# Scans with a gate: moving VectorE's half gate by one product, and loading the gate's z chunks earlier into a ring of six

## The chip, the cores and the metric

The kernel runs on one core of one Trainium2 chip, in one launch. The metric is the device time of that launch in microseconds (us), taken as the median of several runs. The kernel of before takes 9846.35 us (three runs, 9833.42 to 9846.51). The profiled run that all lines below come from took 9824.87 us, with a span of 9823.0 us from the first to the last instruction.

## The reference, cut to what matters

Layer 0 is an attention block on an image batch of 8 x 128 x 128 x 128; its output feeds layer 1. Layer 1 is a two-dimensional selective scan. Its last part is what the change touches:

```python
delta = softplus(dt_weight[k] @ dt + dbias)          # per direction k of four
dA    = exp(delta * A)
xc    = dA * xc + (delta * u) * B                    # the scan, step by step over L = 16384
y     = xc * C
y     = y0 + y1 + y2 + y3                            # four directions, plus u * D
yz    = y * silu(z)                                  # the gate
yn    = gamma * (yz - mean) / sqrt(var + 1e-5) + beta
out   = yn @ Wout
```

There are 8 images, 256 inner channels (two halves of 128 partitions), and four scan directions for each image. silu(z) was computed in layer 0 and lies in HBM as `zs`.

## The kernel before

The program has three stages, one after the other: layer 0, the front of layer 1, and the scans (`layer1_scan`). The change is in the scans alone, which begin at about 5000 us and run to the end.

One *step* handles one chunk of 1024 positions of one direction of one image, both channel halves. 16 chunks make a direction (`NCH`), four directions make an image, 8 images follow each other: 512 steps, numbered n. The four directions of an image add into one tile `y` that stays in SBUF. The first direction of an image (place 0) writes `y`, so while it runs, the finished `y` of the image before must leave, chunk by chunk, just ahead of the writes. These 16 steps of each image are called *leaving steps* here; `leaving[n]` names the chunk that leaves in step n. Of the other places, two write `y` in turned order (the turned steps).

Nothing is left to a scheduler: `in_order` ties each engine's instructions to the order in which `step(n)` writes them. The order of one leaving step of before is:

- VectorE: `emit(n-1, 0)` and `emit(n-1, 1)` (the two products state x C of the step before, L917), `scan(n, 0)` (L889/L891), eight instructions of `store` for the chunk that left in the step before (L1019), `scan(n, 1)`, `state` (L899), `variance` (L1001), then its half of the gate for the next chunk (`gate(*soon, 1, nc.vector)`, L968).
- GpSimd (POOL): `weigh(n, 0)` (delta x u, L882), `deviation` (L1005, L1006), `weigh(n, 1)`, its own half of the gate for the next chunk (L968), and in some steps the issue of a DMA that adds the D term into `y` (`add_d`, L844).
- ScalarE (ACT): two `decay` (exponentials, L879), two squares of gated values (L971), a copy, two `soften` (softplus, L875), with a table load ahead of each kind.
- TensorE (PE): `moments` (L981), `delta` for step n+1 (L871), `to_tokens`, `spread` (L905), and `project` (32 matrix products, L1013), which reads both halves of z and writes into the PSUM tile that `scan(n, 1)` has finished with.
- The sync engine's queue (SP), which issues nearly all DMAs, in order, each after the semaphores that it waits for: `load_rows(n+2)` (L853, L854), `load(n+3)` (L860), the two `store` DMAs out<-r (L1023), and last the two `fetch` DMAs z<-zs (L964).

The buffers that matter: `z` is a ring of five tiles, and a chunk takes two, from `fetch` until `project` has read them. `r`, the output tile of `store`, is a ring of two, and both are used in every leaving step, so the store of a step needs the out DMAs of the step before to have landed. `sp` (the softplus result) is a ring of three. `px` in PSUM is a ring of three.

The schedule of the fetches before is written as

```python
fetched[n + j - 2 if j > 1 else n + j - 4] = e
```

where n is the image's first leaving step and j the number of the chunk: chunks 0 and 1 are fetched four and three steps ahead of the first leaving step, the others at the end of the step two ahead of their own.

Of the kernel before, what the change touches and what calls it, by code (L numbers as in the profile page):

```python
# [8 lines left out]
F32 = mybir.dt.float32  # L9
# [7 lines left out]
P = 128  # L17
# [4 lines left out]
NC2 = 2  # L22
R = 8
K = 4
GW = 4
GN = GW * H
# [3 lines left out]
CH = 1024  # L30
CW = CH // H
NCH = L // CH
# [7 lines left out]
def split3(nc, parts, x):  # L40

    for j in range(3):
        nc.vector.tensor_copy(parts[j], x)
        if j < 2:
            nc.vector.tensor_tensor(x, x, parts[j], ALU.subtract)
# [642 lines left out]
def layer1_scan(ctx: ExitStack, tc, ubs, xps, zs, gs, dtw, dtb, a_log, gamma, beta, w_out, out):  # L688
# [15 lines left out]
    nc = tc.nc  # L704
    const = ctx.enter_context(tc.tile_pool(name="l2c", bufs=1))
    big = ctx.enter_context(tc.tile_pool(name="l2b", bufs=1))
    wp = ctx.enter_context(tc.tile_pool(name="l2w", bufs=3))
# [14 lines left out]
    D2 = 2 * P  # L722
    wparts = dram.tile([3, R, K, D2], BF16, name="wparts")
    bparts = dram.tile([3, K, D2], BF16, name="bparts")
    for dst, src, rows in ((wparts, dtw.rearrange("k r d -> r k d"), R), (bparts, dtb.rearrange("o (k d) -> o k d", d=D2), 1)):
        x = wp.tile([rows, K, D2], F32, name="w32", tag="sp", bufs=3)
        nc.sync.dma_start(x, src)
        q = wp.tile([rows, 3, K, D2], BF16, name="w16", tag="ub", bufs=4)
        split3(nc, [q[:, j] for j in range(3)], x)
        for j in range(3):  # L730
            if rows == 1:
                nc.sync.dma_start(dst[j : j + 1], q[:, j])
            else:
                nc.sync.dma_start(dst[j], q[:, j])
# [8 lines left out]
    for i in range(3):  # L743
        t = const.tile([P, CH], BF16, name=f"rows{i}")
# [3 lines left out]
    for i in range(2):  # L748
        t = const.tile([P, D2], BF16, name=f"dtw{i}")
# [23 lines left out]
            nc.vector.memset(sel[at : at + 1, hf, j : j + 1], 1.0)  # L773
    pb = pe.tile([P, P], F32, name="pbw", tag="pt")
    for c in range(NC2):
        bt = wp.tile([P, P], F32, name="bt", tag="z", bufs=5)
        nc.vector.tensor_copy(bt, gb[:, 1, c : c + 1].to_broadcast([P, P]))
        nc.tensor.matmul(pb, bt, wg[:, c, :], start=(c == 0), stop=(c == NC2 - 1))
    bw = const.tile([P, P], F32, name="bw")
# [59 lines left out]
    ubt, sp, da, st = {}, {}, {}, {}  # L839
# [6 lines left out]
    def load_rows(n):  # L846
        sl, i = units[n]
        m = sl.at(i)
        rw = rws[n % 3]
        md = NCH - 1 - m if sl.dt_turned_back else m  # L850
        src = xps[sl.dt_image, sl.dt_order].rearrange("j r l -> (j r) l")
        for j in range(3):
            nc.sync.dma_start(rw[3 * NR * j : 3 * NR * j + 3 * NR, :], src[:, md * CH : md * CH + CH])  # L853
        nc.sync.dma_start(rw[96:99, :], xps[sl.b, sl.order, :, R + 1, m * CH : m * CH + CH])  # L854

    def load(n):
        sl, i = units[n]
        m = sl.at(i)
        ubt[n] = wp.tile([P, NC2, CH], F32, name="ubt", tag="ub", bufs=4)
        nc.sync.dma_start(ubt[n], ubs[sl.b, sl.order].rearrange("c p l -> p c l")[:, :, m * CH : m * CH + CH])  # L860
# [10 lines left out]
            nc.tensor.matmul(p[:, hf * 512 : hf * 512 + 512], sl.dw[:, c * P : c * P + P], src, start=True, stop=True)  # L871

    def soften(n, c):
        sp[n, c] = t = wp.tile([P, CH], F32, name="sp", tag="sp", bufs=3)
        nc.scalar.activation(t, da[n, c], AF.Softplus)  # L875

    def decay(n, c):
        sl, i = units[n]
        nc.scalar.activation(da[n, c], sp[n, c], AF.Exp, scale=sa[:, sl.s, c : c + 1])  # L879

    def weigh(n, c):
        nc.gpsimd.tensor_tensor(ubt[n][:, c, :], ubt[n][:, c, :], sp.pop((n, c)), ALU.mult)  # L882
# [24 lines left out]
    def emit(n, hf):  # L907

        sl, i = units[n]
        h = ubt[n][:, :, hf * 512 : hf * 512 + 512]
        c = cps.pop((n, hf)).to_broadcast([P, NC2, GN])
        if sl.place == 0:
            v = sl.y_at(i, hf)
            split = "p c (a b) -> p c a b"
            nc.vector.tensor_tensor(v, h.rearrange(split, b=H), c.rearrange(split, b=H), ALU.mult)  # L917
            if hf == 1:
                ubt.pop(n)
            return  # L920
        if hf == 1:
            nc.vector.tensor_tensor(h, h, c, ALU.mult)  # L922
            return
        p = da.pop((n, 1))
        if sl.y_turned:
            ts[n] = p.rearrange("p (c b a) -> p c b a", c=NC2, a=GW)
            t = p.rearrange("p (c b a) -> p c a b", c=NC2, a=GW)
            split = "p c (a b) -> p c a b"
            nc.vector.tensor_tensor(t, h.rearrange(split, b=H), c.rearrange(split, b=H), ALU.mult)  # L929
        else:  # L930
            t = p.rearrange("p (c q) -> p c q", c=NC2)
            ts[n] = t.rearrange("p c (a b) -> p c a b", b=H)
            nc.vector.tensor_tensor(t, h, c, ALU.mult)  # L933

    def gather(n):

        sl, i = units[n]
        v = sl.y_at(i, 0)
        if sl.y_turned:
            v = v.rearrange("p c a b -> p c b a")  # L940
        nc.vector.tensor_tensor(v, v, ts.pop(n), ALU.add)  # L941
# [9 lines left out]
    zt, rst, pts, mv = {}, {}, {}, {}  # L951

    def piece(m, hf):
        return y[:, :, (2 * m + hf) * GN : (2 * m + hf + 1) * GN]

    def mirrored(o, m, hf):
        p = 2 * m + hf
        return 2 * NCH - 1 - p if o % 2 == 1 else p

    def fetch(o, m):  # L960
        for hf in range(2):
            zt[m, hf] = z = wp.tile([P, NC2, GN], F32, name="z", bufs=5)
            p = mirrored(o, m, hf)
            nc.sync.dma_start(z, zs[o].rearrange("c p l -> p c l")[:, :, p * GN : p * GN + GN])  # L964

    def gate(o, m, hf, eng):
        z, ym = zt[m, hf], piece(m, hf)
        eng.tensor_tensor(z, ym[:, :, ::-1] if o % 2 == 1 else ym, z, ALU.mult)  # L968

    def square(m, hf):  # L970
        nc.scalar.activation(piece(m, hf), zt[m, hf], AF.Square)  # L971
# [31 lines left out]
    def deviation(m):  # L1003
        rstd = rst[m]
        nc.gpsimd.tensor_scalar(rstd, rstd, 0.0, EPS1, ALU.max, ALU.add)  # L1005
        nc.gpsimd.tensor_tensor(rstd, rstd, half, ALU.pow)  # L1006
# [20 lines left out]
    leaving, summed, fetched = {}, {}, {}  # L1027
    for o in range(B):
        n = (o + 1) * K * NCH
        for j in range(NCH):  # L1030
            e = o, NCH - 1 - j if o % 2 == 1 else j
            leaving[n + j] = e
            fetched[n + j - 2 if j > 1 else n + j - 4] = e
            summed[n - NCH + 3 + (3 * j + 1) // 2] = e
    N = len(units)

    def step(n):
        live = 0 <= n < N
        then = n + 1 < N
        before = 1 <= n <= N  # L1040
        now, last, soon = (leaving.get(n + i) for i in (0, -1, 1))
        first = before and units[n - 1][0].place == 0
        if before:
            emit(n - 1, 0)
            if not first:
                gather(n - 1)
            emit(n - 1, 1)
        if n + 2 < N:
            load_rows(n + 2)
        if first and n + 3 < N:  # L1050
            load(n + 3)
        if live:
            for c in range(NC2):
                decay(n, c)
            weigh(n, 0)
        if last:
            deviation(last[1])
        if live:
            weigh(n, 1)
        if now:  # L1060
            for hf in range(2):
                square(now[1], hf)
            moments(now[1])
        if live:
            scan(n, 0)
            da.pop((n, 0))
        if last:
            for hf in range(2):
                store(*last, hf)
        if then:  # L1070
            for c in range(NC2):
                delta(n + 1, c)
        if now:
            keep(now[1])
        if then:
            for c in range(NC2):
                soften(n + 1, c)
        if now:
            to_tokens(now[1])
            square_mean(now[1])  # L1080
        if live:
            scan(n, 1)
            state(n)
        if now:
            variance(now[1])
        if live:
            spread(n, 0, "pc")
            spread(n, 1, "pt")
        if soon:
            gate(*soon, 0, nc.gpsimd)  # L1090
            gate(*soon, 1, nc.vector)
        if now:
            p = da.pop((n, 1)) if live else px.tile([P, CH], F32, name="px")
            for hf in range(2):
                project(now[1], hf, p[:, hf * 512 : hf * 512 + 512])
        elif live and units[n][0].place == 0:
            da.pop((n, 1))
        if before and not first:
            add(n - 1)
        if n + 3 < N and not first:  # L1100
            load(n + 3)
        if live and units[n][1] == 1 and n - 1 + NCH < N:
            units[n - 1 + NCH][0].weights()
        if n in summed:
            add_d(*summed[n])
        if n in fetched:
            fetch(*fetched[n])

    with in_order(tc):
        units[0][0].weights()  # L1110
# [74 lines left out]
```

## Time and profile before

| what | value |
|---|---|
| median of 3 runs | 9846.35 us |
| VectorE busy, whole span | 8276.1 us (84%) |
| GpSimd busy | 7184.2 us (73%) |
| ScalarE busy | 7129.7 us (73%) |
| TensorE busy | 6386.5 us (65%) |
| DMA moved | 1851.21 MB, 188 GB/s over the span |
| VectorE's half gate (L968) | 128 instructions, mean 2233 ns |
| GpSimd's half gate (L968) | 128 instructions, mean 2380 ns |

Busy shares over the whole span mix three stages. What a change in the scans is worth is read from the windows of the scans, and there from the leaving steps apart from the turned ones. In a timeline line the columns are start, duration, engine, line, operation, output<-inputs, shape and count; in brackets stands how long the engine was idle before it, and what ended that.

### The profile page before, as it was taken

What the parts mean: (1) busy time and instruction counts of PE and PEld (TensorE: products, weight loads), DVE (VectorE), ACT (ScalarE), POOL (GpSimd) and SP (SyncE); (2) the same over time, 40 slices, a digit from 0 to 9 for tenths busy, and PEclk for the clock granted to TensorE, in tenths of its full rate; (3) what the DMA queues carried; (4) which work ended last, traced back from release to release, by engine and by line L of the source; (5) the groups of instructions that cost most, each with busy time, mean ns of one, the idle gap of its engine ahead of it and who ended that gap; (6) DMA issues with size and microseconds to landing.
All of it is one profiled execution on the core that took longest, in us unless ns stands there. A gap on an engine that the chain in (4) does not pass through costs nothing. (4 is left out here: it accounts for less than half of the span.)

```text
span 9823.0 us, 89967 instructions
## 1 busy us (share of the span) xinstructions
PE 6386.5 (65%) x24352; PEld 3135.3 (32%) x24352; DVE 8276.1 (84%) x8676; ACT 7129.7 (73%) x8226; POOL 7184.2 (73%) x4352
## 2 busy tenths in 40 slices
PE   8999999988787678667823544636345363553636
PEld 5555555553232223222300311404123040220403
DVE  6557775566898889888979999999999999999996
ACT  5556565556887788777778788887877878787784
POOL 3444554455484578667759899898998989889897
PEclk9999999999898889888955765757557585665857
DMA  2332233323666678877664957759587684866858
GB/s 91 129 131 97 86 118 131 129 101 132 219 221 214 219 265 228 243 248 263 232 197 152 253 177 202 234 164 263 154 223 207 176 257 152 246 185 191 239 153 215
DMA packets 1034807, 1851.21 MB, mean 188 GB/s; under 512 B 274852, under 2 KB 500772, under 8 KB 1026112
## 3 DMA queue, kind: packets, MB, share of 16 engines
q1 hardware_dynamic: 999488, 1711.23, 53.4%
q0 software_dynamic: 34816, 134.23, 7.1%
q8 instruction: 199, 3.26, 0.1%
q14 instruction: 304, 2.49, 0.1%
HBM read 1153.03 MB, written 692.12 MB: 188 GB/s over the span
## 5 line engine op out<-in xcount | busy, mean ns | idle before, releaser
L882 POOL TENSOR_TENSOR ubt<-ubt,sp 128x1024 f32<-128x1024 f32 x1024 | 2451.4, 2441 | 186.3 <-ACT sp L875 159.5
L871 PE MATMUL px<-rows,dtw 128*128 128x512 bf16 x2048 | 948.3, 564 | 2251.9 <-DVE y L941 1011.9
L504 POOL TENSOR_TENSOR tap<-tap 128x1024 f32<-128x1024 f32 x512 | 1206.2, 2366 | 720.7 <-ACT tap L502 614.7
L512 DVE SCALAR_TENSOR_TENSOR acc<-xb,cw,acc 128x1024 f32<-128x1024 f32 x1024 | 1320.7, 1290 | 51.1
L494 PE MATMUL acc<-xi,wt 128*128 128x512 f32 x2048 | 984.3, 625 | 570.8 <-ACT ures L519 570.5
L875 ACT ACTIVATE sp<-px 128x1024 f32<-128x1024 f32 x1024 | 1035.0, 1023 | 405.8 <-PE px L871 263.8
L948 POOL TENSOR_TENSOR y<-y,ubt 128x512 f32<-128x512 f32 x768 | 1160.6, 1548 | 146.4 <-DVE ubt L922 142.8
L871 PEld LDWEIGHTS <-dtw 128*128 128x128 bf16 x2048 | 167.5, 110 | 3071.4 <-issue 963.9
L889 DVE TENSOR_TENSOR_SCAN ubt<-px,state,ubt 128x1024 f32<-128x1024 f32 x480 | 1106.0, 2335 | 4.9 <-issue 3.6
L891 DVE TENSOR_TENSOR_SCAN ubt<-px,state,ubt 128x1024 f32<-128x1024 f32 x480 | 1104.6, 2335 | 6.0 <-issue 3.6
L879 ACT ACTIVATE px<-sp,sa 128x1024 f32<-128x1024 f32 x1024 | 1103.3, 1109 | 6.1
L502 ACT ACTIVATE tap<-xb,cw 128x1024 f32<-128x1024 f32 x768 | 833.2, 1139 | 155.4 <-DVE acc L510 92.4
L875 ACT ACT_TABLE_LOAD x512 | 656.9, 1283 | 223.7 <-PE px L871 205.8
L274 POOL TENSOR_TENSOR q<-q,qs 128x512 f32<-128x512 f32 x256 | 270.9, 1058 | 674.0 <-DVE qs L273 672.8
L494 PEld LDWEIGHTS acc<-xi,wt 128*128 128x128 f32 x2048 | 395.8, 199 | 1139.0 <-ACT ures L519 676.0
L879 ACT ACT_TABLE_LOAD x512 | 656.9, 1283 | 9.0
L1013 PEld LDWEIGHTS px<-wg,z 128*128 128x128 f32 x4096 | 586.3, 228 | 163.9 <-issue 157.9
L905 PE MATMUL pc<-rows,csel 128*128 128x512 bf16 x1024 | 515.9, 584 | 128.0 <-DVE rstd L1001 125.2
L1013 PE MATMUL px<-wg,z 128*128 128x128 f32 x4096 | 585.3, 312 | 0.0
L467 PE MATMUL pxb<-xi,wi 128*128 128x512 f32 x1024 | 497.4, 608 | 29.1 <-ACT xh L607 24.7
L941 DVE TENSOR_TENSOR y<-y,px 128x1024 f32<-128x1024 f32 x384 | 468.6, 1220 | 14.2
L922 DVE TENSOR_TENSOR ubt<-ubt,pc 128x1024 f32<-128x1024 f32 x384 | 466.2, 1214 | 0.0
(158 smaller groups left out, 15026.4 us busy)
## 6 DMA issues: line engine op xcount, KB each, us to landing
ubt<-ubs SPq DMA_DIRECT2D x512, 1024.0 KB
zs<-z SPq DMA_DIRECT2D x512, 256.0 KB
ubs<-ures SPq DMA_DIRECT2D x256, 512.0 KB
ubs<-turned SPq DMA_DIRECT2D x256, 512.0 KB
y<-gs POOLq DMA_DIRECT2D x128, 1024.0 KB, 11.9
z<-zs SPq DMA_DIRECT2D x256, 512.0 KB
rows<-xps SPq DMA_DIRECT2D x1536, 60.0 KB
xi<-x SPq DMA_DIRECT2D x120, 576.0 KB
```

The costliest lines, as they stand in the source:

```text
L494: nc.tensor.matmul(acc[:, s, :], wt[:, j, c, :], x, start=(j == 0), stop=(j == len(ON_PE) - 1))
L502: nc.scalar.activation(t, at(n, c, *d), AF.Copy, scale=cw[:, c, tap(*d) : tap(*d) + 1])
L504: nc.gpsimd.tensor_tensor(sums[n, c], sums[n, c], t, ALU.add)
L512: nc.vector.scalar_tensor_tensor(acc, at(n, c, *d), cw[:, c, tap(*d) : tap(*d) + 1], acc, ALU.mult, ALU.add)
L871: nc.tensor.matmul(p[:, hf * 512 : hf * 512 + 512], sl.dw[:, c * P : c * P + P], src, start=True, stop=True)
L875: nc.scalar.activation(t, da[n, c], AF.Softplus)
L879: nc.scalar.activation(da[n, c], sp[n, c], AF.Exp, scale=sa[:, sl.s, c : c + 1])
L882: nc.gpsimd.tensor_tensor(ubt[n][:, c, :], ubt[n][:, c, :], sp.pop((n, c)), ALU.mult)
L889: nc.vector.tensor_tensor_scan(e[:, ::-1], x[:, ::-1], e[:, ::-1], start, ALU.mult, ALU.add)
L891: nc.vector.tensor_tensor_scan(e, x, e, start, ALU.mult, ALU.add)
L948: nc.gpsimd.tensor_tensor(v[:, c], v[:, c], h[:, c], ALU.add)
L1013: nc.tensor.matmul(po[:, w, :], z[:, c, w * H : w * H + H], wg[:, c, :], start=(c == 0), stop=(c == NC2 - 1))
```

## The change

It has four parts. VectorE's half of the gate moves out of the end of the step before (`soon`) into the step in which the chunk leaves (`now`), between the two products `emit(n-1, 0)` and `emit(n-1, 1)`. The z ring grows from five tiles to six, so that three whole chunks fit; the softplus ring shrinks from three to two, which pays for it in SBUF. The fetches of an image's first three chunks move to the last turned-order direction, 20 to 18 steps ahead of the first leaving step; the others are fetched one step earlier than before. And the place of `fetch` in the step moves from the very end to the front, after `load_rows` and (in steps that follow a place-0 step) `load`. It is meant to take the gate away from GpSimd's product, to have z there in time, and to move some of the loads into steps where the DMA engines are less used.

```diff
@@ bt, in the setup of the stage: tag="z", bufs=5 -> 6; w32: tag="sp", bufs=3 -> 2
     def soften(n, c):
-        sp[n, c] = t = wp.tile([P, CH], F32, name="sp", tag="sp", bufs=3)
+        sp[n, c] = t = wp.tile([P, CH], F32, name="sp", tag="sp", bufs=2)
...
     def fetch(o, m):
         for hf in range(2):
-            zt[m, hf] = z = wp.tile([P, NC2, GN], F32, name="z", bufs=5)
+            zt[m, hf] = z = wp.tile([P, NC2, GN], F32, name="z", bufs=6)
...
-            fetched[n + j - 2 if j > 1 else n + j - 4] = e
+            fetched[n + j - (3 if j > 2 else NCH + 4)] = e
...
             emit(n - 1, 0)
             if not first:
                 gather(n - 1)
+        if now:
+            gate(*now, 1, nc.vector)
+        if before:
             emit(n - 1, 1)
         if n + 2 < N:
             load_rows(n + 2)
         if first and n + 3 < N:
             load(n + 3)
+        if n in fetched:
+            fetch(*fetched[n])
         if live:
             for c in range(NC2):
                 decay(n, c)
...
         if soon:
             gate(*soon, 0, nc.gpsimd)
-            gate(*soon, 1, nc.vector)
...
         if n in summed:
             add_d(*summed[n])
-        if n in fetched:
-            fetch(*fetched[n])
```

More of the change, by code (lines that the diff above doesn't have):

```diff
@@ L725, in layer1_scan @@
     for dst, src, rows in ((wparts, dtw.rearrange("k r d -> r k d"), R), (bparts, dtb.rearrange("o (k d) -> o k d", d=D2), 1)):
-        x = wp.tile([rows, K, D2], F32, name="w32", tag="sp", bufs=3)
+        x = wp.tile([rows, K, D2], F32, name="w32", tag="sp", bufs=2)
         nc.sync.dma_start(x, src)
@@ L775, in layer1_scan @@
     for c in range(NC2):
-        bt = wp.tile([P, P], F32, name="bt", tag="z", bufs=5)
+        bt = wp.tile([P, P], F32, name="bt", tag="z", bufs=6)
         nc.vector.tensor_copy(bt, gb[:, 1, c : c + 1].to_broadcast([P, P]))
```

## The prediction

> **What bounds the kernel now.** I read four views, in this order: the page for the stage, the windows for the kind of step, the timelines of single engines inside one image's leaving steps, and the waits. From the page, the slices:
>
> ```profile
> DVE  6557775566898889888979999999999999999996
> DMA  2332233323666678877664957759587684866858
> ```
>
> Each digit is a fortieth of the span, 246 us. From slice 21 on (the scans) VectorE is at 9, while the DMA digit swings between 4 and 9. The windows say what swings; a line gives start:end, length, busy time of PE, PEld, DVE, ACT and POOL, then TensorE clock, DMA share and GB/s:
>
> ```profile
> 5200.00:5380.00 180.00, 63.77 (x132) 15.10 (x132) 178.28 (x131) 148.24 (x133) 171.76 (x89) 0.50 0.49 152
> 5380.00:5486.00 106.00, 37.62 (x78) 8.43 (x78) 105.04 (x78) 87.40 (x78) 100.50 (x59) 0.50 0.80 207
> 5530.00:5711.00 181.00, 136.17 (x933) 99.99 (x933) 170.64 (x225) 137.99 (x150) 152.10 (x82) 0.92 0.92 267
> ```
>
> The first window is turned steps: VectorE 99% busy, DMA engines half idle. The second is the last direction of an image, with the D-term loads, DMA 0.80. The third is leaving steps: VectorE 94%, DMA 0.92. The start of each step's first scan gives the length of steps: 8.21 us in turned ones whatever the image; over seven images (the eighth leaves after the last scan) the means by position in the leaving phase are 10.6 and 10.8 for the two steps ahead of it, 14.7 for the first, 11.65 for the second, 12.17 for the third to fourteenth (11.4 to 14.0), 11.7, 9.2. Only these steps can change much.
>
> What they lose today shows in VectorE's and GpSimd's timelines:
>
> ```profile
> 5600.97 1.21 DVE L968 TENSOR_TENSOR z<-y,z 128x1024 f32<-128x1024 f32 x1
> 5611.80 3.90 DVE L968 TENSOR_TENSOR z<-y,z 128x1024 f32<-128x1024 f32 x1
> ```
>
> ```profile
> 5611.84 2.76 POOL L882 TENSOR_TENSOR ubt<-ubt,sp 128x1024 f32<-128x1024 f32 x1
> 5614.18 1.62 POOL L1005 TENSOR_SCALAR rstd<-rstd 128x8 f32<-128x8 f32 x1
> ```
>
> The same gate takes 1.21 us or 3.90: in the second case it overlaps GpSimd's product L882, and ends about 1.1 us after GpSimd lets go. The row's mean is 2233 ns, so about 1.0 us of each gate is such a wait. Next, the sync queue:
>
> ```profile
> 5607.86 1.38 SPq L1023 DMA_DIRECT2D out<-r  x2
> 5609.35 6.83 SPq L964 DMA_DIRECT2D z<-zs  x2
> 5616.22 2.43 SPq L853 DMA_DIRECT2D rows<-xps  x3
> ```
>
> The second z load stands 6 us in the queue until `project` has released its buffer, and the next rows stand behind it. The out DMAs, ahead of it, don't. Last, the waits from 5000 us on (total, times, longest), and the sync queue's own in 5516 to 5711:
>
> ```profile
> PE px L871 <- DVE r L1019: 133.5, 104, 4.4
> POOL z L968 <- DMA z<-zs: 86.8, 31, 5.0
> DVE z L968 <- DMA z<-zs: 48.6, 27, 4.1
> DVE r L1019 <- DMA out<-r: 16.4, 9, 4.5
> ```
>
> ```profile
> SPq L964 <- PE px L1013: 47.8, 13, 6.9
> ```
>
> Late z costs something today; a store waiting for its output tile (the third kind, L1019 for out<-r) almost nothing, 16.4 us in all. PE's L871 waiting for L1019 says that `delta` of the next step can't start before the store is done.
>
> [...]
>
> **The change part by part.**
>
> *Gate between the products.* After `variance` VectorE now runs `emit(n-1,0)`, 1.21 us, without contention, while GpSimd finishes L882. Then the gate comes at about L882's end and takes 1.2. So I take 1.0 us off each leaving step whose length VectorE sets. `square`, which needs the gate, comes on ScalarE behind two decays (2.15 us), so 1.2 us of delay for the gate is hidden there.
>
> *Softplus ring of two.* `soften(n+1,0)` then needs `weigh(n,0)` done, `soften(n+1,1)` needs `weigh(n,1)`. In turned steps GpSimd ends the second product of a step at 6009.43 and ScalarE's second softplus of the next step begins at 6012.59; in leaving steps likewise, as the softplus comes behind the first scan or the store. Cost 0, hidden by the scans.
>
> *First three chunks in turned steps.* One step there moves 1.25 MB (152 GB/s x 8.21 us), the DMA share is 0.49, and 1.05 MB more makes it about 0.9. Rows are loaded two steps ahead, so cost 0. In return the two steps ahead of the leaving phase lose their queue of z, rows and D-term loads: 10.6 to 8.2, and 10.8 to about 9.6 (the moved gate still falls ahead of the next scan). That is 3.6 us an image, x8 = 29 us. The z waits go too (27 us of VectorE's idle time in leaving steps).
>
> *Place of the fetch.* Here the cost is. In before, the z loads of a step stood last. In the changed kernel, by the order of its instructions, `fetch` of chunk j+3 stands in step n = first + j ahead of the out DMAs of that step, and its tiles are those of chunk j, which `project` reads at the end of this very step. A ring of six holds j, j+1, j+2; the early place asks for a seventh and eighth tile. So the sync queue stands on z until `project(n)` ends, and the two out DMAs stand behind it. On them waits the next step's store (r ring of two), which stands on VectorE between the two scans; behind it are scan 1, variance, and PE's delta. Steps with fetch: j = 3..15, so outs are held in the second to thirteenth leaving step, and stores stall in the third to fourteenth: 12 steps an image.
>
> The new cycle of such a step, from the trace of before:
> 1. Store end to end of `project`: scan 2.33, state and variance about 0.4, then project starts (5598.53 to 5601.32 = 2.8 us). Project takes 3.73 or 5.35 us; over 112 of them about 4.6 in the mean. Sum 7.4.
> 2. End of project to the out DMAs issued: semaphore, second z issue 0.38, out issue 0.37: about 0.9.
> 3. Landing. Before shows no out behind two z loads. Of the 256 outs, by the landing times in the trace, the fastest take 1.9 us, a quarter under 4.0, the median 5.8. Bounds: 2.9 (light queue, with half a z load ahead), 5.8 (the median, which had 1 MB of ubt ahead). I take 4.0[...].
> 4. Store: 2.13 us of L1019, the second half just after its out has landed. 2.13.
>
> Sum 14.4 us against 12.17: +2.2 x 12 x 7 images = +188 us. With the low bound and project at 3.73: 6.5 + 0.9 + 2.9 + 2.13 = 12.4, +0.3 x 84 = +22. With the high: 8.1 + 0.9 + 5.8 + 2.13 = 16.9, +4.8 x 84 = +400. In these steps the gate's 1.0 us is no gain: VectorE waits there anyway. It stays a gain in first, second and fifteenth steps: 3 x 1.0 x 7 = 21 us. In the eighth image, where nothing is scanned any more (9670 to 9823), a z load earlier and an out later about cancel: 0.
>
> Total: +188 - 29 - 21 = +138, so about 9985 us.
>
> **The rivals.**
> - *Out lands in time (not slower).* For it: the store now begins 2.1 us after project's end in the median and needs the out there; if landing took under 3 us, the cycle is 12.4 and the sum 22 - 50 = -28: about 9820, on the edge of what can be told. Against it: only a tenth of the outs landed in under 2.45 us.
> - *The queue doesn't matter (faster).* If I misread which `project` the z loads wait for, the gate's 1.0 x 15 x 7 = 105, z waits 27 and the 29 above would come to some -160: 9690. Against it: the waits of the changed program name the product of the same step.
> - *DMA congestion (much slower).* D-term loads share the engines in 7 of 16 leaving steps; with every out at the median or worse, +400 - 50: 10190. For it: DMA share 0.92 today. Against it: longer steps thin the queue.
>
> **How the numbers follow.** Held outs at 14.4 us a step 0.65; congestion 0.15; outs just in time 0.12; queue harmless 0.08. The likeliest gives 9985. The range takes the held outs with cycles of 12.9 to 16.1 us, that is landing from 2.5 to 5.8 us in place of 4.0: (0.7 or 3.9) x 84 less 50, about 9860 to 10130. Slower: 0.65 + 0.15 and a part of the in-time case, 0.82; same 0.06; faster 0.12.
>
> **What would show it.** Right: L1019 waiting for out<-r becomes a top wait of VectorE, some 2 to 4 us in each of about 84 steps; out<-r issues in the sync queue come after L964 and after project; L968 on VectorE falls to about 1.2 to 1.5 us; z waits vanish; the steps before the leaving phase shrink to 8.2 and 9.6. Wrong: L1019 starts without a wait in leaving steps, or steps of 11 us there; or turned steps longer than 8.21, which would put the fault on the softplus ring.

## The result, and the profile after

The changed kernel takes 10307.33 us (median of four runs, 10303.99 to 10317.81); the kernel before took 9839.89 us beside it. The ratio is 1.0477, with an interval of 1.0459 to 1.0495. It is slower by some 467 us, the way that was forecast, but more than three times as much as the 138 us of the forecast, and outside its range.

The two rows of slices from the page of the changed kernel that answer to those of before:

```profile
DVE  6556666657888988889797896988969879799795
DMA  2333222325675688876657566575675765747657
```

VectorE's 9 of the scans now has holes (5 to 8), about one for each image. The DMA row, which stood at 7 to 9 in most of the leaving slices of before, doesn't pass 7 there: VectorE and the DMA engines both stand for a part of the time. From the waits of the changed kernel, from 5000 us to its end (total us, times, longest):

```profile
DVE r L1019 <- DMA out<-r: 628.4, 100, 15.6
PE px L871 <- DVE r L1019: 537.3, 91, 14.9
DVE rstd L1001 <- ACT mv L997: 94.6, 119, 5.9
```

The store's wait for its output tile went from 16.4 us to 628.4. TensorE waits behind it in turn, 537 us where it was 133.5. The waits for z are gone. What the sync queue itself waits for, in the first leaving phase of the changed kernel (5530 to 5791 us; in that of before it was 47.8, 13, 6.9):

```profile
SPq L964 <- PE px L1013: 153.4, 26, 20.4
```

One held step in the timeline of the changed kernel shows the whole cycle:

```profile
5624.14 2.34 DVE L889 TENSOR_TENSOR_SCAN ubt<-px,state,ubt 128x1024 f32<-128x1024 f32 x1
5624.28 1.01 PE L871 MATMUL px<-rows,dtw 128*128 128x512 bf16 x2 [5.72 <-DVE r L1019]
...
5627.64 5.44 PE L1013 MATMUL px<-wg,z 128*128 128x128 f32 x32
...
5631.34 2.17 SPq L964 DMA_DIRECT2D z<-zs  x2
...
5633.91 0.83 SPq L1023 DMA_DIRECT2D out<-r  x2
...
5639.04 2.16 DVE L1019 SCALAR_TENSOR_TENSOR r<-px,rstd,bw 128x128 f32<-128x128 f32 x8 [6.01 <-DMA out<-r]
```

The store before this stretch ended at about 5624.2. `project` runs until 5633.1; the second z load goes at 5633.15, the out DMAs right behind it, though the store that filled their tiles had ended more than nine us earlier. The next store starts when they have landed, at 5639.04.

Where the time went, from the starts of the first scans in the two traces, means over seven images: the third to fourteenth leaving steps grew by 63.9 us an image (209.9 against 146.0), x7 = 447. The steps on either side (two ahead of the phase, its first two and last two, and the one behind it) grew by 2.0 x 7 = 14. The last image's phase, in which nothing is scanned, went from 155 to 177 us. The turned steps are 8.21 us as before. Most of the rest of the 493 us between the two profiled spans lies ahead of the scans, where the program is the same: they begin at 5003 us in one and at 5016 in the other.

Within the 447, two sorts of step. Ten of the twelve take 16.7 to 17.0 us, one 17.7 (a single long step in one image), and the third leaving step 23.9, which the forecast didn't have. Its lines in the timeline of the changed kernel:

```profile
5542.77 2.17 SPq L964 DMA_DIRECT2D z<-zs  x2
...
5547.46 0.98 SPq L860 DMA_DIRECT2D ubt<-ubs  x1
...
5555.04 1.77 SPq L1023 DMA_DIRECT2D out<-r  x2
...
5571.83 2.16 DVE L1019 SCALAR_TENSOR_TENSOR r<-px,rstd,bw 128x128 f32<-128x128 f32 x8 [15.59 <-DMA out<-r]
```

and the windows of the same stretch (after the length: busy PE, PEld, DVE, ACT, POOL, then TensorE clock, DMA share, GB/s):

```profile
5523.00:5543.00 20.00, 10.51 (x51) 6.63 (x52) 16.23 (x10) 10.30 (x12) 12.74 (x8) 0.60 0.41 98
...
5546.00:5573.00 27.00, 10.12 (x68) 6.00 (x65) 10.23 (x15) 12.14 (x13) 16.32 (x9) 0.81 0.89 242
```

In the first leaving step the sync queue stands on its first blocked z load for 20 us and issues nothing, with the DMA engines 0.41 busy; then two steps' loads, two D-term loads and the outs all go within some 17 us, and the outs issued at 5555 land at about 5572.

### The profile page after: what moved, and what is told of

It reads as the page before. It is cut to its first block, busy times and chain, and to the rows that moved or that the text cites. A ratio compares the mean times of both kernels' runs of the same rounds, so it can differ in the third digit from the quotient of the medians.

```text
span 10316.0 us, 90031 instructions
## 1 busy us (share of the span) xinstructions
PE 6563.0 (64%) x24352; PEld 3276.3 (32%) x24352; DVE 8205.8 (80%) x8676; ACT 7148.8 (69%) x8226; POOL 7125.6 (69%) x4352
## 4 chain that ended last, share of the span: by engine, by line
DVE 31%; PE 10%; DMA 6%; issue 2%; ACT 1%; SPq 0%; POOL 0%; DVEq 0%; ACTq 0%; POOLq 0%
DVE ubt L891 8%; DVE ubt L889 8%; PE px L1013 6%; DMA out<-r 5%; DVE y L941 4%; DVE ubt L922 4%; DVE px L929 3%; DVE r L1019 2%; PE pq L993 1%; DVE px L933 1%; PE pm L981 1%; PE px L871 1%; PE pc L905 1%; DVE state L899 1%; DMA rows<-xps 0%
## 5 line engine op out<-in xcount | busy, mean ns | idle before, releaser
L882 POOL TENSOR_TENSOR ubt<-ubt,sp 128x1024 f32<-128x1024 f32 x1024 | 2452.0, 2449 | 432.0 <-ACT sp L875 416.1
L871 PE MATMUL px<-rows,dtw 128*128 128x512 bf16 x2048 | 986.1, 583 | 2613.3 <-DVE y L941 1035.6
L948 POOL TENSOR_TENSOR y<-y,ubt 128x512 f32<-128x512 f32 x768 | 1147.6, 1530 | 170.9 <-DVE ubt L922 166.9
L1019 DVE SCALAR_TENSOR_TENSOR r<-px,rstd,bw 128x128 f32<-128x128 f32 x1024 | 276.8, 343 | 655.9 <-DMA out<-r 628.4
L1013 PEld LDWEIGHTS px<-wg,z 128*128 128x128 f32 x4096 | 672.0, 257 | 116.8 <-issue 107.5
L1013 PE MATMUL px<-wg,z 128*128 128x128 f32 x4096 | 665.2, 339 | 0.0
L905 PE MATMUL pc<-rows,csel 128*128 128x512 bf16 x1024 | 543.7, 611 | 62.6 <-DVE rstd L1001 57.4
```

Of the source, the lines that this page charges most:

```text
L948: nc.gpsimd.tensor_tensor(v[:, c], v[:, c], h[:, c], ALU.add)
L1013: nc.tensor.matmul(po[:, w, :], z[:, c, w * H : w * H + H], wg[:, c, :], start=(c == 0), stop=(c == NC2 - 1))
```

## The experiments

Each time is a median, each ratio is to the kernel before, measured beside it (9838 to 9843 us).

**Which wait holds the outs.** Three runs take the blocked queue apart.

```diff
 # e2_one_step_later: the changed kernel, and
-            fetched[n + j - (3 if j > 2 else NCH + 4)] = e
+            fetched[n + j - (2 if j > 2 else NCH + 4)] = e
```

> The changed kernel with the fetch at the front of the step, ahead of the out DMAs, as changed, but chunks 3 to 15 one step later, so that their tiles are those of a chunk whose product was in the step before. Theory (it is the wait for the product of the same step that holds the outs): leaving steps of 11 to 12 us, about 9730 us. Rival (outs suffer because 1 MB of z data goes ahead of them in the DMA rings, wherever the wait is): the store still waits 2 us or more for out<-r in most leaving steps, over 10000 us.

Measured: 9820.18 us, ratio 0.9981 (0.9974 to 0.9988). One character takes back all of the 467 us and a little more. The z loads still stand ahead of the outs in the queue; only what they wait for is a step older. So it is the wait for the product of the same step. The 11 to 12 us came about (11.4 to 12.3 from the third to the fourteenth) in all but the fourth leaving step (15.5). There the rival has its part: the outs ahead of it stand behind two z halves and an ubt load and beside a D-term load, all issued within some 3 us, and in the second leaving phase they landed about 14 us after their issue. The store's waits in that step come to 31 us in all.

```diff
 # e4_place_alone: the kernel before, and
+        if n in fetched:                 # front of the step, after load
+            fetch(*fetched[n])
...
-        if n in fetched:                 # end of the step
-            fetch(*fetched[n])
```

> The kernel before with the place of the fetch alone changed: front of the step; ring of five, softplus ring of three, gate and fetch steps as before. With five tiles the second half of a chunk still needs the first tile that the product of the same step frees. Theory: the outs are held in the same way, leaving steps of 15 to 17 us, 10150 to 10350 us. Rival (the place is harmless, the six-tile ring or the gate makes the cost): within 0.5% of 9840 us.

Measured: 10021.87 us, 1.0185 (1.0170 to 1.0200), leaving steps of 13.7 to 15.8 us from the third on. The place alone costs, and less than expected. I put that down to the ring of five, which has a free tile for the first half, so that only the second waits; no run tests this.

```diff
 # e6_place_r_four: e4_place_alone, and
-        r = wp.tile([P, GW, P], F32, name="r", bufs=2)
+        r = wp.tile([P, GW, P], F32, name="r", bufs=4)
 # softplus ring 3 -> 2
```

> The place of the fetch alone, as in that run (10022 us there), with an output ring of four in place of two (and the softplus ring of two, which pays for it). The out DMAs are held just as long, but the store needs only those of two steps before. Theory (VectorE's wait in the store is what costs): the store's wait for out<-r under 60 us (335 there), 9800 to 9870 us. Rival (the blocked sync queue costs by what else stands behind it, rows and ubt): stays over 9950 us.

Measured: 9797.40 us, 0.9958 (0.9945 to 0.9971). VectorE's wait for out<-r is gone from the waits. The sync queue still stands behind `project` (73 us from 5516 to 5711, 126 in e4_place_alone, 47.8 before); with tiles to spare, no store waits for it. The link from the queue to the time is the store's two tiles. The third to fourteenth leaving steps are back at 12.17 us, the mean of before. What this kernel gains over before comes mostly from the way into the leaving phase, see "Early z" below.

```diff
 # e1_fetch_last: the changed kernel, fetch moved back to the end of the step
```

> The changed kernel with one thing put back: the fetch stands at the very end of the step, behind the out DMAs, as before; ring of six, early first chunks, gate between the products and softplus ring of two stay. Theory (outs held behind a z load that waits for the product of the same step): the store's wait for out<-r falls from some 630 us in the scans to under 40 us, the third to fourteenth leaving steps go from 16.6-17.7 us (23.9 the third) to about 11, and the time falls under the kernel before: about 9720 us. Rival (the cost is the gate's new place, the ring of two, or the z loads in turned steps): stays above 10200 us.

Measured: 9921.95 us, 1.0084 (1.0069 to 1.0099). Most of the loss goes, but the time doesn't fall under that of before, and the number missed by 200 us. With the fetch last, this step's outs go free, but both halves now wait for the product (one did before), and the next step's rows, ubt and outs stand behind them: out waits of 181.7 us remain, and the steps from the third to the fourteenth take 11.7 to 16.0 us. The place isn't enough to mend it; the index is.

**Why a held step takes 16.8 us and not 14.4.** The pause of 5.72 us in front of TensorE's second delta looked like the reason: the same two matrix products take 1.01 us behind it and 0.60 where other products end just ahead of them (5617.95 in the same trace).

```diff
 # e5_busy_pe: the changed kernel; keep moved ahead of delta, and
             delta(n + 1, 0)
+            if now:
+                warm(now[1])             # ten products into a bank that nobody reads
             delta(n + 1, 1)
 # e10_busy_pe_half: five products
```

> The changed kernel with ten needless matrix products a leaving step on TensorE, between the two products of delta, at the time at which TensorE would stand idle for the store (they write a PSUM bank that nothing reads). Theory (the idle time of 5.7 us before the second delta lowers TensorE's clock, and the cycle of a held step is longer than forecast mostly because project, delta and to_tokens run at half clock): project goes from 5.4 to about 3.8 us and the held steps from 16.8 to about 14.5 us, the whole to about 10120 us. Rival (project is long for another reason, as DMA or the weights' loads): project stays at 5.4 us and the time at 10300 us or longer.

> As the run with ten needless products, with five (4.4 us of TensorE by that run's trace, in place of 8.8), so that they end before the store does. Theory (the held steps are long because TensorE cools while it waits for the store): project 3.7 us in place of 5.4 in the changed kernel, held steps about 14.5 us in place of 16.8, the whole about 10130 us. Rival (the clock is a side effect; what sets the step is the landing of the outs): steps stay over 16 us and the time within 1% of 10307 us.

Measured with ten: 10581.09 us, 1.0752 (1.0736 to 1.0768). The products take 8.77 us, longer than the pause of 5.72 that they were to fill, so TensorE is late itself and every step takes 18.55; but `project` is 3.73 us in all of the held ones. With five: 10206.35 us, 1.0374 (1.0360 to 1.0387). From its timeline (`project` is L1019 there, delta L872, the store L1025):

```profile
5662.40 2.16 DVE L1025 SCALAR_TENSOR_TENSOR r<-px,rstd,bw 128x128 f32<-128x128 f32 x8 [4.41 <-DMA out<-r]
...
5664.61 0.59 PE L872 MATMUL px<-rows,dtw 128*128 128x512 bf16 x2 [0.44 <-DVE r L1025]
...
5667.35 3.73 PE L1019 MATMUL px<-wg,z 128*128 128x128 f32 x32
```

and one window of each, first the changed kernel, then the one with five products (the number after the busy times is the TensorE clock):

```profile
5600.00:5700.00 100.00, 64.50 (x357) 47.80 (x350) 61.38 (x90) 55.84 (x60) 57.54 (x34) 0.69 0.73 208
```

```profile
5600.00:5700.00 100.00, 86.62 (x455) 46.35 (x460) 68.09 (x103) 60.92 (x66) 61.24 (x36) 0.96 0.80 229
```

A kernel with more work in it is 101 us faster. The clock goes from 0.69 to 0.96 (what the expectation calls cooling is this granted clock), and the held steps (fourth to fourteenth) from 16.9 to 15.3 us. The expected 14.5 wasn't reached: `project` is 3.73 us in half of the steps, but 4.3 in the mean, and landing is no shorter. By the starts of the first scans the held steps give 123 us, and the products cost some 63 in the steps that aren't held. The third leaving step gives another 52 us (from 23.9 to 16.4), which isn't the clock's doing alone: the two steps ahead of it are 2.5 to 3.0 us longer here, and what piled up has that time to land (argued, not tested). The trace of the changed kernel shows the clock behind such a pause: TensorE is idle for 5.8 us up to 5641 and then stands at 0.50, in the same columns as above (how short a pause would do isn't shown):

```profile
5641.00:5647.00 6.00, 5.73 (x24) 4.79 (x24) 5.53 (x7) 4.20 (x5) 2.66 (x3) 0.50 0.25 101
```

**The third leaving step.**

```diff
 # e14_fourth_chunk_later: the changed kernel, chunk 3 fetched with chunk 4, one step later
```

> The changed kernel with chunk 3 alone fetched one step later, together with chunk 4, so that the sync queue doesn't stand for some 20 us in the first leaving step; from the second leaving step on, outs are held as in the changed kernel. Theory (the third leaving step takes 23.9 us because two steps' loads pile up behind that first wait and land 16 us after their issue): that step falls to about 17 us, the others stay at 16.7, about 10255 us. Rival (the ten loads of dtw in the second leaving step make it): the third step stays over 22 us, 10300 us.

Measured: 10260.23 us, 1.0430 (1.0416 to 1.0444); the third leaving step takes 16.4 us, the held ones 16.6 to 17.5. The pile-up was the first wait's doing; the ten loads of dtw are still there.

**What the gate is worth.**

```diff
 # e3_gate_alone: the kernel before, gate(*now, 1, nc.vector) between the products
 # e11_moments_first: e2_one_step_later, to_tokens and square_mean ahead of
 #                    delta(n + 1, 1) and soften(n + 1, 1)
```

> The kernel before with the gate's place alone changed (VectorE's half between the two products of the step in which the chunk leaves); rings of five and three, fetches as before. Theory (the gate's wait for GpSimd goes, but most of it comes back as a wait for the variance's mean from ScalarE, and the first gate of an image waits some 6 us behind GpSimd): within 0.7% of 9840 us, the wait of variance for mv grows from 55 to some 100 us over the leaving steps. Rival (the forecast's reading: 1.0 us off every leaving step): about 9740 us.

> The run with the fetches one step later (9820 us), and the products that turn the means to tokens, with the square of the mean, put ahead of the second delta and the second softplus on TensorE and ScalarE. Theory (the gate's new place frees VectorE of its wait for GpSimd, and what it gains comes back as a wait of variance for the mean's square): that wait falls from 112 us over the leaving steps to under 40, and the time to about 9750 us. Rival (VectorE isn't what sets these steps, the next wait takes its place): within 0.3% of 9820 us.

Measured: e3_gate_alone 9829.63 us, 0.9991 (0.9983 to 0.9999); e11_moments_first 9795.00 us, 0.9958 (0.9945 to 0.9972). In e3_gate_alone the gate's own time falls by 46 us (285.8 to 240.3, or 2233 to 1877 ns each), and variance's wait for the mean grows by 23 (81.3 to 104.7). The other half isn't accounted for here. In e2_one_step_later that wait is longer still, from its waits from 5000 us on:

```profile
DVE rstd L1001 <- ACT mv L997: 134.1, 109, 5.6
...
DVE r L1019 <- DMA out<-r: 88.3, 32, 9.3
```

Putting the mean first takes that wait to 45.6 us, but the time falls by 25 us and not by 70: the rival's number. Why, the rows of the gate in e11_moments_first show:

```profile
L968 POOL TENSOR_TENSOR z<-y,z 128x1024 f32<-128x1024 f32 x128 | 308.1, 2407 | 0.8 <-PE pm L981 0.8
L968 DVE TENSOR_TENSOR z<-y,z 128x1024 f32<-128x1024 f32 x128 | 279.1, 2181 | 0.0
```

VectorE's gate is back at 2181 ns, where the changed kernel has 1566 and the kernel before 2233. I put that down to the gate coming early again and meeting GpSimd's L882; the row shows its length and not the cause. The third to fourteenth leaving steps took 12.17 us in the mean before, and 11.85 at the least in any run, with the gate where it was (e7_early_z_alone, below).

```diff
 # e13_all_mended: e6_place_r_four, gate between the products, means first
```

> The run with the fetch in front and an output ring of four (9797 us), with the gate between the products and the means' products ahead of the second delta. Theory: with no store held and no wait for the mean, the gate's 1.0 us a leaving step is a gain: about 9710 us. Rival (GpSimd or the DMA engines are the next bound): within 0.3% of 9797 us.

Measured: 9804.59 us, 0.9968 (0.9955 to 0.9980), no better than e6_place_r_four, and the gate is at 2539 ns. The rival's number holds, though not which of its two engines is the bound. Neither order of VectorE's work got the 1.0 us a step.

**Early z, and the first gate.**

```diff
 # e7_early_z_alone: the kernel before, rings of six and two, first three chunks 20 to 18 steps ahead
 # e9_both_mended: e2_one_step_later, the first gate of an image back at the end of the step before
```

> The kernel before with the ring of six, the softplus ring of two and the first three chunks in the turned steps; gate and the fetch's place at the end of the step as before, the other chunks two steps ahead as before. Forecast's reading: the two steps ahead of the leaving phase fall from 10.6 and 10.8 to 8.2 and 9.6 us and z waits go, 9790 to 9815 us. Rival (the first gate's wait behind GpSimd, which late rows hid before, gives it back): within 0.2% of 9840 us. A softplus ring that costs would show as turned steps over 8.22 us.

> The run with the fetches one step later (9820 us), and the first gate of each image put back at the end of the step ahead of the leaving phase; the other fifteen stay between the products. Theory (that first gate stands some 6 us behind two GpSimd instructions in the new place): the step ahead of the leaving phase falls from 15.3 to about 10 us, the one after it may give back up to 3; 9780 to 9800 us. Rival (the 6 us are a wait that moves elsewhere, as the kernel before has them one step later): no change from 9820 us.

Measured: e7_early_z_alone 9818.07 us, 0.9976 (0.9968 to 0.9984), between the two expectations; e9_both_mended 9816.43 us, 0.9983 (0.9975 to 0.9991), its rival. In both, as in the changed kernel, the second step ahead of the leaving phase falls from 10.6 to 8.2 us, and the step next to the phase grows: 10.8 before, 15.3 changed, 17.7 in e7_early_z_alone and 15.4 in e9_both_mended. The timeline of the changed kernel shows what stands there:

```profile
5522.13 7.13 DVE L968 TENSOR_TENSOR z<-y,z 128x1024 f32<-128x1024 f32 x1
5522.65 3.23 POOL L882 TENSOR_TENSOR ubt<-ubt,sp 128x1024 f32<-128x1024 f32 x1
5524.95 3.22 POOL L968 TENSOR_TENSOR z<-y,z 128x1024 f32<-128x1024 f32 x1
```

The gate starts at 5522.13 and ends at 5529.26, 1.1 us after GpSimd's whole run of instructions. The same gate in the kernel before:

```profile
5508.77 3.47 POOL L948 TENSOR_TENSOR y<-y,ubt 128x512 f32<-128x512 f32 x2
5509.70 1.40 DVE L968 TENSOR_TENSOR z<-y,z 128x1024 f32<-128x1024 f32 x1
```

There rows came late (TensorE stood for 8.0 us, up to 5498.4, until they had landed), and GpSimd had stood still for 3.8 us shortly before. The gate met the first of GpSimd's two short instructions of L948 and got in between them; the second then took 2.25 us in place of 1.25. With z loaded early GpSimd doesn't stand still (no idle time from 5509.4 to 5528.2 in the changed kernel) and is further on when the gate comes. It can go either way in one and the same kernel: in e9_both_mended it waited 9.7 us in five of the seven images and 2.0 and 1.7 in the other two, where the step took 9.9 and 9.7 us.

Early z isn't the only way to shorten the step two ahead. In e4_place_alone and e6_place_r_four, with z as late as before and the gate at the end of the step, it takes 8.4 and 8.5 us, and the first gate 1.42 (GpSimd stands still for 1.3 and 1.4 us there). The three steps from two ahead to the first leaving one then come to 31.7 us, against 36.1 before, 35.2 in the changed kernel and 38.5 in e7_early_z_alone. Times seven this is 31 us, three quarters of what e6_place_r_four gains. What e7_early_z_alone gains comes from the third to fourteenth leaving steps (142.2 us an image against 146.0), not from the steps of its expectation.

## Why the forecast was right in direction and wrong in size

- *Place of the fetch, held outs:* right, and shown by e2_one_step_later (the wait), e6_place_r_four (the two tiles) and e4_place_alone (the place alone).
- *The cycle of a held step:* this is the step that failed, by size. Over the fourth to thirteenth leaving steps the trace of the changed kernel gives: store end to project 3.4 us (forecast 2.8), project 5.5 (4.6), to the outs issued 0.9 (0.9), landing 4.8 (4.0), store 2.1 (2.1), and 0.1 between. Sum 16.8, not 14.4. Of the 2.4 us, 1.5 lie in the first two terms, and I put them down to TensorE's clock (0.69 from 5600 to 5700 us, 0.92 before): I had taken `project` as the mean of before, though the very stall that was forecast leaves TensorE standing; e10_busy_pe_half shows 2.8 and 4.3 in those two terms. Another 0.8 is landing. The first out lands 0.8 us behind the second z half in the mean, and that half takes 4.9 us from its issue; the forecast's 4.0 us was an estimate of mine, between the 1.9 of the fastest out before and the median of 5.8. No run takes this term apart. 2.4 x 84 steps = 202 us.
- *The third leaving step:* missed. I counted each held step alone, and not what the first wait lets pile up. 7.0 us over the others x 7 = 49; e14_fourth_chunk_later shows the cause.
- *First chunks in turned steps, 29 us:* wrong. The 2.4 us of one step came (8.21 us), the next step gave back 4.5, as the gate met GpSimd, and the first leaving step fell by 3.0 (14.7 to 11.7): 0.9 us an image, 6 us in all. That turned steps have room for the loads was right, 8.21 us in all of them.
- *Gate, 21 us in the steps not held:* not seen in the second and fifteenth (11.65 and 11.7 before, 11.7 and 11.9 now); the 3.0 us of the first can't be told from those of z. That the gate would fall to 1.2 to 1.5 us was right but for the first gate of each image: the mean of all 128 fell from 2233 to 1566 ns, that of the first seven images without their first gates to 1233. But variance then waits for the mean (94.6 us against 81.3), and where that is mended the gate takes 2181 ns again.
- *Softplus ring of two, cost 0:* right; turned steps 8.21 us in e7_early_z_alone and the changed kernel alike.
- *The eighth image, 0:* wrong by 22 us; its outs are held too. In e2_one_step_later that phase takes 148.5 us.
- *Rivals:* outs in time and a harmless queue are both refuted by the waits. The congestion rival's 10190 us was nearest in size, but the longer cycle isn't mainly congestion: the DMA share is 0.70 from 5600 to 5770 us, under the 0.92 of before (5530 to 5711). The third leaving step, with two D-term loads in its pile-up and a share of 0.89, is of its kind.

Not tried: an output ring of four with the z ring of six (no run shows whether SBUF holds both), and a chunk order that gives GpSimd a pause at the first gate.

## What to carry to other kernels

A load that is issued early in program order, but into a buffer which a later instruction of the same step frees, held up here what stood behind it in its queue (the queue stood on z for 153.4 of 261 us in the changed kernel's first leaving phase, and a wait for the product of one step earlier gave the 467 us back); count the live tiles at the point of issue, and see what else stands in that queue. When a forecast stall feeds back into the engine that ends it, take that engine's speed after such a pause and not its mean (`project`: 5.5 us, and not 4.6). A gain on the busiest engine is worth only what its partners leave: in e3_gate_alone the gate's row fell by 46 us, the wait for the mean grew by 23, and the kernel's time stayed within 0.2%.

## What the runs showed of the hardware

- The record of VectorE's half gate could last not through one GpSimd instruction but through a run of them (7.13 us in all in the changed kernel, where its median is 1.22; a mean of 9.7 at this place in e7_early_z_alone). By the records the gate had started 0.5 us ahead of the second L882 of the run and still ended behind it and the L968 that followed, and in the forecast's own line it started 0.04 us ahead of the L882 that it outlasted. VectorE's products L917, nearly all of them beside GpSimd's instructions, took 1.21 to 1.22 us in all 256 instances of either trace. Nor is the long wait a rule: the gate got in between two GpSimd instructions without a pause in the kernel before (L948, 1.40 us) and in e3_gate_alone (L882, 2.2 us), in all seven images of each. What decides isn't shown. In the run GpSimd's instructions have longer records (3.2 us for 2.35), but they start 2.3 us apart, so GpSimd lost no pace.
- A needless 4.5 us of matrix products in each leaving step raised TensorE's granted clock from 0.69 to 0.96 (5600 to 5700 us) and took 1.6 us off each held step, as `project` fell from 5.5 to 4.3 us in the mean.
